# The first routed tile's up-projections placed between layer 0's last averages, and its rows joined in a side step

## The chip, the cores and the metric

The kernel runs on one core of a Trainium2 chip. The core's engines work side by side, each on its own queue: TensorE (PE) multiplies matrices, VectorE (DVE) and ScalarE (ACT) do elementwise work and read results out of PSUM, GpSimd (POOL) copies within SBUF and issues gathers and scatters by DMA, SyncE (SP) issues most of the other DMAs. The metric is device time in microseconds (us); a lower time is better.

## The reference

The program is two layers on 2 x 2048 tokens of width 256, in float32. Each layer adds to x an attention and a feed-forward part, both computed from the same normalised input. Only layer 0 is touched by the change; cut to what matters, it is:

```python
xn = _layernorm(x)
# causal attention, one head of width 256
q, k, v = xn @ Wq.T + bq, xn @ Wk.T + bk, xn @ Wv.T + bv
attn = where(causal, -inf, q @ k.T) / sqrt(256)
att = softmax(attn) @ v
# experts: 8 routed ones (hidden width 512), of which each token uses 2, and 2 shared ones
scores = softmax(xn @ gate_w + gate_b)
weights, indices = top_k(scores, 2)
expert = lambda x, e: (silu(x @ w1[e] + b1[e]) * (x @ w2[e] + b2[e])) @ w3[e] + b3[e]
routed = sum(weights * expert(xn, indices))
x = x + att + mean_of_shared_experts(xn) + routed
```

Layer 1 has the same attention without biases but with an output projection, and in place of the experts a block that works on the 255 highest-scoring tokens of each sequence.

## The kernel before, in words

**Attention of layer 0.** The queries are cut into tiles of 128. A tile is written (b, i): sequence b, block i of 16. The order is (0,0) to (0,15), then (1,15) down to (1,0), so the last tiles are the shortest. For each tile `scores` multiplies queries and keys on PE in chunks of 512 keys into PSUM banks of the tags `sc` and `tr` (two buffers each), DVE masks and shifts them (L264, L266), ACT takes the exponential (L274). Then `turn` transposes the probabilities without PE: POOL splits each float32 into two 16-bit planes (`planes`, L305), SP has a DMA transpose them (`across`, L307), and `join` puts the halves together again, one on DVE (L285) and one on ACT (L286), giving `pT`. `average` multiplies `pT` by the values on PE (L320), in a bank of the tag `pv`, and DVE adds the result to x (L330). Averages run some tiles behind their scores, in the list `pending`; when all tiles are scored, three are left: (1,2), (1,1) and (1,0). The loop `for late in pending` does these three.

**Side work.** Between pieces of the attention, `beside` takes steps of a generator, `side0`: it normalises the later blocks (`prepare0`), routes the tokens (`route_experts`), scatters the rows of all tokens to `sorted_x` in the order of their experts, and fetches the weights and rows of the first two routed tiles (`fetch(0)`, `fetch(1)`). In the last part of the attention it takes 0.72 steps a piece.

**Routed experts.** A tile is 256 places of `sorted_x` that belong to one expert; eight half tiles of 128 take what is left over. `fetch(t)` loads the expert's number into a register (L652), has SP transpose the rows by DMA into `xs` (L657), and loads the weights `rw1`, `rw2`, `rw3` (L665) and the biases `be` (L669), each with two buffers. `run(t)` joins the two 16-bit halves of the rows into `xT` on POOL (L765), and multiplies: for each of two pairs of hidden chunks a group of four products with `w1` into a bank `sc` and a group of four with `w2` into a bank `tr` (L772), four groups in all. ACT applies Silu (L780), DVE multiplies (L781), giving `hid`, and the down-projection follows on PE (L788). `xT`, `act`, `hid` and `y` come from the pool `hp`, which is opened when the attention's pools are closed.

**The order of work.** The Python code traces the instructions in program order. A planner then simulates the program and sets the order of each engine's queue: what is ready first goes first, and of what is ready what was traced first. So an instruction can stand on its engine ahead of others that were traced before it: the load of tile 2's expert number, traced in `run(2)`, ran at 322.1 us, in the middle of the attention. `tc.add_manual_dep(i, other, order, ...)` fixes that i stays behind another instruction of its engine, and with `wait` in place of `order` i also waits for it across engines. `lead(i)` marks the last instruction of the main work on an engine, in `main`; `behind` ties what a side step traces to it: POOL's instructions wait for the marked DVE instruction, SP's stay behind the marked SP one. `chained` keeps the SP instructions of all fetches in their order among themselves.

Of the kernel before, what the change touches and what calls it, by code (L numbers as in the profile page):

```python
# [17 lines left out]
P = 128  # L18
# [7 lines left out]
TT = 256  # L26
# [24 lines left out]
def transformer_kernel(ctx: ExitStack, tc: tile.TileContext, a: dict, out: bass.AP):  # L51
# [15 lines left out]
    def bank(tag):  # L67
        return psum.tile([P, 512], F32, tag=tag, name=f"ps_{tag}")
# [40 lines left out]
    def lead(i):  # L109

        main[i.ins.engine] = i.ins
# [121 lines left out]
                nc.tensor.transpose(ps[:, j * P : (j + 1) * P], xn[:, j, c * P : (c + 1) * P], ident)  # L233
            evacuate(xnT[g][:, c, :], ps)

    def attention(pool, tiles, project_q, values, each, shifts=None):

        def scores(b, i):
            g0 = b * BPB
            qT = queries[g0 + i // 4]
            row = pool.tile([P, S], F32, tag="row", name="row")
            mx = small.tile([P, 4], F32, tag="mx", name="mx")
            n = (i + 1) * P  # L250
            chunks = [(c, min(512, n - c)) for c in range(0, n, 512)]
            for k, (c, w) in enumerate(chunks):
                ps = bank(("sc", "tr")[k % 2])
                for dc in range(2):
                    product = nc.tensor.matmul(  # L255
                        ps[:, :w],
                        lhsT=qT[:, dc, (i % 4) * P : (i % 4 + 1) * P],
                        rhs=xnT[g0 + k][:, dc, :w],
                        start=(dc == 0),
                        stop=(dc == 1),  # L260
                    )
                lead(product)
                if c + w == n:
                    nc.vector.tensor_add(ps[:, w - P : w], ps[:, w - P : w], tri)  # L264
                by = 1.0 / 16.0 if shifts is None else shifts[g0 + i // 4][:, i % 4 : i % 4 + 1]
                lead(nc.vector.tensor_scalar(  # L266
                    row[:, c : c + w], ps[:, :w], by, None,
                    op0=ALU.mult if shifts is None else ALU.add, op1=ALU.max, accum_out=mx[:, k : k + 1],
                ))
                piece()  # L270
            nmx = small.tile([P, 1], F32, tag="nmx", name="nmx")
            nc.vector.tensor_reduce(nmx, mx[:, : len(chunks)], AX.X, ALU.max, negate=True)
            total = small.tile([P, 1], F32, tag="total", name="total")
            lead(nc.scalar.activation(row[:, :n], row[:, :n], AF.Exp, bias=nmx, accum_out=total))  # L274
            inv = small.tile([P, 1], F32, tag="inv", name="inv")
            nc.vector.reciprocal(inv, total)
            return b, i, row, inv, chunks

        def join(k, w, across, turned):

            pT = pool.tile([P, 512], F32, tag="pT", name="pT", bufs=6)
            words = pT[:, :w].bitcast(U16).rearrange("p (n k) -> p n k", k=2)
            flat = across.rearrange("p b n -> p (b n)")
            for i in (
                nc.vector.tensor_copy(words[:, :, 1], flat[:, :w]),  # L285
                nc.scalar.copy(words[:, :, 0], flat[:, w : 2 * w]),  # L286
            ):
                tc.add_manual_dep(i.ins, main[i.ins.engine].name, order, reason="not before it is there")
            turned[k] = pT

        def piece():

            pieces[0] += 1
            while joins and joins[0][0] <= pieces[0]:
                join(*joins.pop(0)[1:])
            beside()

        def turn(b, i, row, inv, chunks):

            turned = [None] * len(chunks)  # L300
            for k, (c, w) in enumerate(chunks):
                halves = row[:, c : c + w].bitcast(U16).rearrange("p (n k) -> p n k", k=2)
                planes = pool.tile([P, 1024], U16, tag="planes", name="planes", bufs=4)
                for h in range(2):
                    nc.gpsimd.tensor_copy(planes[:, h * w : (h + 1) * w], halves[:, :, 1 - h])  # L305
                across = pool.tile([P, 8, P], U16, tag="across", name="across", bufs=4)
                lead(nc.sync.dma_start_transpose(across[:, : 2 * w // P, :], planes[:, : 2 * w]))  # L307
                joins.append((pieces[0] + LAG + k, k, w, across, turned))
                if len(joins) == 4:
                    join(*joins.pop(0)[1:])  # L310
            return b, i, turned, inv, chunks

        def average(b, i, turned, inv, chunks):
            g0 = b * BPB
            pv = bank("pv")
            for k, (c, w) in enumerate(chunks):
                while turned[k] is None:
                    join(*joins.pop(0)[1:])
                for j in range(0, w, P):
                    product = nc.tensor.matmul(  # L320
                        pv[:, :D],
                        lhsT=turned[k][:, j : j + P],
                        rhs=values[g0 + k][:, j // P, :D],
                        start=(c + j == 0),
                        stop=(c + j == i * P),
                    )
                lead(product)
                piece()
            xt = x_blocks[g0 + i // 4][:, i % 4, :]
            nc.vector.scalar_tensor_tensor(xt, pv[:, :D], inv, xt, op0=ALU.mult, op1=ALU.add)  # L330

        queries = {}
        pending, joins, pieces = [], [], [0]
        def meet(tile):

            each(*tile)
            g = tile[0] * BPB + tile[1] // 4
            if g not in queries:
                queries[g] = project_q(g)

        meet(tiles[0])
        for tile, later in zip(tiles, tiles[1:] + [None]):
            pending.append(turn(*scores(*tile)))
            if later:
                meet(later)
            while sum(len(p[2]) for p in pending[:-1]) >= 3:
                average(*pending.pop(0))
        for late in pending:
            average(*late)


    in_turn = [(0, i) for i in range(S // P)] + [(1, i) for i in reversed(range(S // P))]
# [11 lines left out]
    with ExitStack() as l0:  # L364
# [279 lines left out]
        def fetch(t):  # L644
# [30 lines left out]
            fetched[t] = *parts, be, xs  # L675
            yield

        def side0():
            for blocks in (range(1, BPB), range(BPB, NB)):
                yield from moments(blocks)  # L680
                for g in blocks:
                    yield from prepare0(g)
            yield from route_experts()
            rows_ctx.close()
            wp.append(experts_ctx.enter_context(tc.tile_pool(name="experts", bufs=2, side="right")))
            for t in range(2):
                yield from fetch(t)

        def before_tile(b, i):
            while values[b * BPB + i // 4] is None:  # L690
# [6 lines left out]
            for _ in work_of:  # L697
                pass
        side.append(side0())
        attention(work, in_turn, project_q0, values, before_tile, shifts)  # L700
        assert next(clearing, None) is None
        while side:
            step()
# [46 lines left out]
    with ExitStack() as moe:  # L750
        hp = moe.enter_context(tc.tile_pool(name="routed", bufs=2))

        def run(t):
# [3 lines left out]
                    pass  # L757
            w1, w2, w3, be, xs = fetched[t]
            b1, b2, b3 = be[:, 0:4], be[:, 4:8], be[:, 8:]

            xs = xs.rearrange("p c n -> p (c n)")[:, : 4 * n].rearrange("p (c n) -> p c n", n=n)
            xT = hp.tile([P, 2, TT], F32, tag="xT", name="xT", bufs=3)[:, :, :n]
            words = xT.bitcast(U16).rearrange("p c (n k) -> p c n k", k=2)
            for k in range(2):
                nc.gpsimd.tensor_copy(words[:, :, :, 1 - k], xs[:, 2 * k : 2 * k + 2, :])  # L765
            hid = hp.tile([P, 4, TT], F32, tag="hid", name="hid")[:, :, :n]
            for h in range(0, 4, 2):
                p1, p2 = bank("sc"), bank("tr")
                for ps, we_in in ((p1, w1), (p2, w2)):
                    for k in range(2):  # L770
                        for dc in range(2):
                            nc.tensor.matmul(  # L772
                                ps[:, k * n : (k + 1) * n],
                                lhsT=we_in[:, dc, (h + k) * P : (h + k + 1) * P], rhs=xT[:, dc, :],
                                start=(dc == 0), stop=(dc == 1),
                            )
                for k in range(2):
                    act = hp.tile([P, TT], F32, tag="act", name="act", bufs=3)[:, :n]
                    at, hc = slice(k * n, (k + 1) * n), slice(h + k, h + k + 1)
                    activated = nc.scalar.activation(act, p1[:, at], AF.Silu, bias=b1[:, hc])  # L780
                    nc.vector.scalar_tensor_tensor(  # L781
                        hid[:, h + k, :], p2[:, at], b2[:, hc], act, op0=ALU.add, op1=ALU.mult
                    )
# [762 lines left out]
```

## Time and profile before

| | us |
|---|---|
| median of 3 runs | 1515.09 |
| lowest and highest | 1513.61, 1515.64 |
| profiled execution | 1515.69 |
| its span, first to last instruction | 1514.0 |
| PE busy in the span | 1455.0 (96%) |
| DVE, ACT, POOL busy | 695.7, 440.3, 407.7 |
| first and last average of layer 0 start | 54.5, 346.6 |
| first and last up-projection of a routed tile start | 348.5, 702.7 |
| last down-projection of a routed tile starts | 706.2 |

The profile is of one execution. Its page gives the busy time of each engine, the span in 40 slices (each digit the busy tenths), the DMA queues, the chain of work that ended last, and groups of instructions by line with their count, busy time, mean duration in ns, the idle time of the engine before them and what ended it. The trace behind it can be asked for a stretch of time: busy time by engine, waits, or the instructions in order of time with their start and length, merged where an engine repeats one line. A product of float32 matrices shows as two PE records, so one `average` of three key blocks is "x6", and a group of four up-projections "x8". PEld is PE's load of the stationary operand; SPq is SP's queue, where a DMA's issue is seen.

### The profile page before, as it was taken

The numbers are of one execution on the slowest core, as the hardware profiler recorded it, in microseconds if no ns is written. First come the engines' busy times: TensorE is split into PE (matmuls) and PEld (weight loads), VectorE is DVE, ScalarE is ACT, GpSimd is POOL, SyncE is SP. The second block draws the span as 40 slices with busy tenths as digits, with TensorE's granted clock in tenths as the row PEclk, the third lists the DMA queues.
The fourth block names the chain that finished last, engine by engine and source line by source line (L and its number), as shares of the span: only waits on it lengthen the run. The fifth ranks groups of instructions, "written<-read, shape, count | busy, mean of one in ns | idle before, by whom it ended". The sixth has DMA issues, their size and how long they took to land.

```text
span 1514.0 us, 17838 instructions
## 1 busy us (share of the span) xinstructions
PE 1455.0 (96%) x5796; PEld 1032.3 (68%) x5796; DVE 695.7 (46%) x2068; ACT 440.3 (29%) x831; POOL 407.7 (27%) x597
## 2 busy tenths in 40 slices
PE   6999999998999999999999999999999998999998
PEld 4566666667888888886565656666675765676665
DVE  6347433342222222222433447767556468666344
ACT  2443343332111111111112121125614433344233
POOL 3554776522111111101201222122013123421132
PEclk9999999999999999999999999999999999999999
DMA  4844665575887989873101010220005345621154
GB/s 151 262 113 115 173 147 130 140 154 147 228 224 222 274 237 292 225 218 94 34 18 39 29 56 25 87 71 29 0 21 125 90 87 115 134 51 23 35 118 102
DMA packets 288528, 182.99 MB, mean 121 GB/s; under 512 B 190928, under 2 KB 263376, under 8 KB 288432
## 3 DMA queue, kind: packets, MB, share of 16 engines
q1 hardware_dynamic: 252608, 133.90, 35.8%
q10 hardware_dynamic: 28192, 27.06, 5.8%
q0 software_dynamic: 7632, 20.86, 4.4%
q8 instruction: 48, 0.79, 0.2%
q14 instruction: 48, 0.39, 0.1%
HBM read 93.14 MB, written 45.14 MB: 91 GB/s over the span
## 4 chain that ended last, share of the span: by engine, by line
PE 29%; issue 10%; DVE 7%; POOL 3%; DMA 2%; ACT 2%; POOLq 0%; ACTq 0%; DVEq 0%; SPq 0%
PE ps_tr L1413 6%; PE ps_sc L1413 6%; PE ps_pv L1432 5%; POOL planes L305 3%; DMA across<-planes 2%; PE ps_mm L1284 2%; PE ps_mm L1246 1%; DVE x L1443 1%; PE ps_sc L255 1%; PE ps_mm L876 1%; PE ps_mm L1267 1%; PE ps_pv L320 1%; PE ps_mm L1350 1%; DVE row L266 1%; PE ps_tr L255 1%
## 5 line engine op out<-in xcount | busy, mean ns | idle before, releaser
L305 POOL COPY planes<-row 128x512 uint16<-128x512 uint16 (+3 forms) x320 | 167.1, 569 | 298.9 <-ACT row L274 289.2
L286 ACT COPY pT<-across 128x512 uint16<-128x512 uint16 (+3 forms) x160 | 106.1, 677 | 217.6 <-DMA across<-planes 206.7
L255 PE MATMUL ps_sc<-xnT,qT 128*128 128x512 f32 (+3 forms) x384 | 162.4, 544 | 0.5 <-ACT qT L624 0.5
L781 DVE SCALAR_TENSOR_TENSOR hid<-ps_tr,be,act 128x256 f32<-128x256 f32 (+1 forms) x144 | 61.0, 465 | 186.7 <-PE ps_tr L772 181.7
L1402 POOL DMA_INDIRECT ya<-sorted_y,place x64 | 62.3, 973 | 307.5 <-DVE x L1443 224.3
L780 ACT ACTIVATE act<-ps_sc,be 128x256 f32<-128x256 f32 (+1 forms) x144 | 58.8, 459 | 283.3 <-PE ps_sc L772 283.3
L320 PE MATMUL ps_pv<-v,pT 128*128 128x256 f32 x544 | 128.3, 381 | 6.1 <-ACT pT L286 4.7
L772 PE MATMUL ps_sc<-xT,rw 128*128 128x256 f32 (+1 forms) x576 | 129.5, 368 | 1.6 <-POOL xT L765 1.6
L320 PE MATMUL ps_pv<-vg,pT 128*128 128x256 f32 x544 | 125.1, 381 | 5.4 <-ACT pT L286 5.3
L772 PE MATMUL ps_tr<-xT,rw 128*128 128x256 f32 (+1 forms) x576 | 129.4, 367 | 0.0
L765 POOL COPY xT<-xs 128x512 uint16<-128x512 uint16 (+1 forms) x72 | 49.2, 728 | 293.3 <-DMA xs<-sorted_x 270.7
L788 PE MATMUL ps_pv<-rw,hid 128*128 128x256 f32 x544 | 124.9, 382 | 0.0
L1413 PE MATMUL ps_sc<-xnT,sw 128*128 128x512 f32 x256 | 121.9, 594 | 1.7 <-PEq L816 1.7
L1413 PE MATMUL ps_tr<-xnT,sw 128*128 128x512 f32 x256 | 122.0, 593 | 0.0
L320 PEld LDWEIGHTS ps_pv<-vg,pT 128*128 128x128 f32 x544 | 101.4, 189 | 29.7 <-ACT pT L286 10.3
L320 PEld LDWEIGHTS ps_pv<-v,pT 128*128 128x128 f32 x544 | 101.3, 190 | 28.2 <-ACT pT L286 8.2
L1432 PE MATMUL ps_pv<-sw,hid 128*128 128x256 f32 x512 | 117.5, 380 | 0.0
L772 PEld LDWEIGHTS ps_sc<-xT,rw 128*128 128x128 f32 x576 | 105.3, 190 | 15.4 <-POOL xT L765 2.0
L772 PEld LDWEIGHTS ps_tr<-xT,rw 128*128 128x128 f32 x576 | 105.1, 190 | 13.2
L788 PEld LDWEIGHTS ps_pv<-rw,hid 128*128 128x128 f32 x544 | 99.0, 189 | 19.5 <-DVE hid L781 5.9
L1432 PEld LDWEIGHTS ps_pv<-sw,hid 128*128 128x128 f32 x512 | 96.6, 190 | 18.8 <-issue 6.2
L1420 ACT ACTIVATE act<-ps_sc,sb 128x512 f32<-128x512 f32 x64 | 43.9, 686 | 219.5 <-PE ps_sc L1413 206.4
(332 smaller groups left out, 1964.7 us busy)
## 6 DMA issues: line engine op xcount, KB each, us to landing
rw<-in_rw SPq DMA_DIRECT2D x108, 512.0 KB, 4.5
sorted_x<-zero ACTq DMA_DIRECT2D x13, 768.0 KB, 6.4
sorted_y<-y SPq DMA_DIRECT2D x32, 256.0 KB, 4.1
be<-biases SPq DMA_DIRECT2D x36, 132.0 KB, 4.3
table<-xn SPq DMA_DIRECT2D x8, 514.0 KB, 3.6
x<-in_x SPq DMA_DIRECT2D x8, 512.0 KB, 6.6
gains<-zero ACTq DMA_DIRECT2D x8, 512.0 KB, 3.6
gain<-gains SPq DMA_DIRECT2D x16, 256.0 KB, 2.7
```

Source lines behind the costliest of these rows:

```text
L255: product = nc.tensor.matmul(ps[:, :w], lhsT=qT[:, dc, (i % 4) * P : (i % 4 + 1) * P], rhs=xnT[g0 + k][:, dc, :w], start=(dc == 0), stop=( ...
L286: nc.scalar.copy(words[:, :, 0], flat[:, w : 2 * w]),
L305: nc.gpsimd.tensor_copy(planes[:, h * w : (h + 1) * w], halves[:, :, 1 - h])
L320: product = nc.tensor.matmul(pv[:, :D], lhsT=turned[k][:, j : j + P], rhs=values[g0 + k][:, j // P, :D], start=(c + j == 0), stop=(c + j = ...
L765: nc.gpsimd.tensor_copy(words[:, :, :, 1 - k], xs[:, 2 * k : 2 * k + 2, :])
L772: nc.tensor.matmul(ps[:, k * n : (k + 1) * n], lhsT=we_in[:, dc, (h + k) * P : (h + k + 1) * P], rhs=xT[:, dc, :], start=(dc == 0), stop=( ...
L780: activated = nc.scalar.activation(act, p1[:, at], AF.Silu, bias=b1[:, hc])
L781: nc.vector.scalar_tensor_tensor(hid[:, h + k, :], p2[:, at], b2[:, hc], act, op0=ALU.add, op1=ALU.mult)
L788: product = nc.tensor.matmul(po[:, r, :], lhsT=hid[:, hc, r * P : (r + 1) * P], rhs=w3[:, hc, :], start=(hc == 0), stop=(hc == 3),)
L1402: nc.gpsimd.indirect_dma_start(out=ya, out_offset=None, in_=sorted_y, in_offset=bass.IndirectOffsetOnAxis(ap=place[rank][:, t : t + 1], ax ...
L1413: product = nc.tensor.matmul(ps, lhsT=ww[:, dc, hc * P : (hc + 1) * P], rhs=xnT[g][:, dc, :], start=(dc == 0), stop=(dc == 1),)
L1432: product = nc.tensor.matmul(po[:, :D], lhsT=hid[:, hc, j * P : (j + 1) * P], rhs=w["sw3", n][:, hc, :], start=(hc == 0), stop=(hc == 3),)
```

## The change

A generator `fill_with_first` is passed to layer 0's attention. It yields four times; each time one group of four up-projections of routed tile 0 has been traced. The loop over the last averages takes one group ahead of each of (1,2), (1,1) and (1,0), and one after them. Each group's PE instructions stay behind the average before it, and the next average's first product stays behind the group. `run(0)` then finds its banks filled and begins with Silu. The rows of tile 0 are joined in one more step at the end of `side0`, into a buffer `xT` of the pool `experts` (where the weights are), with one buffer; from tile 1 on they are joined in `run(t)` as before. The PSUM tags and the products are the same.

```diff
-    def attention(pool, tiles, project_q, values, each, shifts=None):
+    def attention(pool, tiles, project_q, values, each, shifts=None, filling=()):
...
                         stop=(c + j == i * P),
                     )
+                    if c + j == 0 and filled_up:
+                        tc.add_manual_dep(product.ins, filled_up.ins.name, order, reason="the filling first")
...
-        for late in pending:
-            average(*late)
+        filling = iter(filling)
+        for late in [*pending, None]:
+            last, n = main[mybir.EngineType.PE], len(nc.cur_bb.bb.instructions)
+            filled_up = next(filling, None)
+            if filled_up:
+                for i in nc.cur_bb.bb.instructions[n:]:
+                    if i.engine == mybir.EngineType.PE:
+                        tc.add_manual_dep(i, last.name, order, reason="not ahead of its turn")
+                lead(filled_up)
+            if late:
+                average(*late)
...
+        def joined(pool, xs, n, bufs):
+            xs = xs.rearrange("p c n -> p (c n)")[:, : 4 * n].rearrange("p (c n) -> p c n", n=n)
+            xT = pool.tile([P, 2, TT], F32, tag="xT", name="xT", bufs=bufs)[:, :, :n]
+            words = xT.bitcast(U16).rearrange("p c (n k) -> p c n k", k=2)
+            for k in range(2):
+                nc.gpsimd.tensor_copy(words[:, :, :, 1 - k], xs[:, 2 * k : 2 * k + 2, :])
+            return xT
+
+        def up(we_in, h, xT, n, tag):
+            ps = bank(tag)
+            for k in range(2):
+                for dc in range(2):
+                    product = nc.tensor.matmul(
+                        ps[:, k * n : (k + 1) * n],
+                        lhsT=we_in[:, dc, (h + k) * P : (h + k + 1) * P], rhs=xT[:, dc, :],
+                        start=(dc == 0), stop=(dc == 1),
+                    )
+            return ps, product
+
+        def fill_with_first():
+            while side:
+                step()
+            w1, w2, _, _, xT = fetched[0]
+            for h in range(0, 4, 2):
+                for we_in, tag in ((w1, "sc"), (w2, "tr")):
+                    first_up[h, tag], product = up(we_in, h, xT, TT, tag)
+                    yield product
...
             for t in range(2):
                 yield from fetch(t)
+            *others, xs = fetched[0]
+            fetched[0] = *others, joined(wp[0], xs, TT, 1)
+            yield
...
-        attention(work, in_turn, project_q0, values, before_tile, shifts)
+        attention(work, in_turn, project_q0, values, before_tile, shifts, fill_with_first())
...
+            if t:
+                xT = joined(hp, xs, n, 3)
...
+                p1, p2 = (
+                    up(we_in, h, xT, n, tag)[0] if t else first_up[h, tag] for we_in, tag in ((w1, "sc"), (w2, "tr"))
+                )
```

More of the change, by code (lines that the diff above doesn't have):

```diff
@@ L333, in attention @@
         pending, joins, pieces = [], [], [0]
+        filled_up = None
         def meet(tile):
@@ L347, in attention @@
                 average(*pending.pop(0))
-        for late in pending:
-            average(*late)
+        filling = iter(filling)
[9 more added lines that the diff above has]
+                average(*late)
+        assert next(filling, None) is None
     in_turn = [(0, i) for i in range(S // P)] + [(1, i) for i in reversed(range(S // P))]
@@ L676, in fetch @@
             yield
+        def joined(pool, xs, n, bufs):
[15 more added lines that the diff above has]
+            return ps, product
+        first_up = {}
+        def fill_with_first():
[6 more added lines that the diff above has]
+                    yield product
         def side0():
@@ L759, in run @@
             b1, b2, b3 = be[:, 0:4], be[:, 4:8], be[:, 8:]
[L761 to L765, printed above, removed]
+            if t:
+                xT = joined(hp, xs, n, 3)
             hid = hp.tile([P, 4, TT], F32, tag="hid", name="hid")[:, :, :n]
             for h in range(0, 4, 2):
[L768 to L776, printed above, removed]
+                p1, p2 = (
+                    up(we_in, h, xT, n, tag)[0] if t else first_up[h, tag] for we_in, tag in ((w1, "sc"), (w2, "tr"))
+                )
                 for k in range(2):
```

## The prediction

> **What bounds the kernel now.** I read the page's slices first, then the costliest groups, then the seam between layer 0's attention and its routed experts: busy time by stretch, waits, and the timeline of each engine. From the page:
>
> ```profile
> PE   6999999998999999999999999999999998999998
> PEclk9999999999999999999999999999999999999999
> L772 PE MATMUL ps_sc<-xT,rw 128*128 128x256 f32 (+1 forms) x576 | 129.5, 368 | 1.6 <-POOL xT L765 1.6
> L788 PE MATMUL ps_pv<-rw,hid 128*128 128x256 f32 x544 | 124.9, 382 | 0.0
> ```
>
> PE is 96% busy, and the routed stage behind the seam has almost no idle time on PE: 1.6 us before the first product, nothing later. So a shift of that stage's start moves its end by as much; what follows (the shared experts) starts behind the routed stage on PE and keeps its own order. What can be won lies where PE has a hole. Busy time of a stretch that starts where average (1,3) has issued its last product (length, then PE, weight load, DVE, ACT, POOL; granted clock, DMA share, GB/s), and the waits around it:
>
> ```profile
> 341.15:348.54 7.39, 3.60 (x15) 2.03 (x13) 3.01 (x9) 1.84 (x6) 2.84 (x7) 1.00 0.13 27
> POOL xT L765 <- PE ps_pv L320: 4.5, 1, 4.5
> PE ps_pv L320 <- ACT pT L286: 2.6, 3, 1.4
> PE ps_sc L772 <- POOL xT L765: 1.6, 1, 1.6
> ```
>
> PE is busy for less than half of 7.39 us. It waits for the turned probabilities of the last small tiles, and then for POOL, whose first join of rows waits for the last average (the pool of `hp` lies where the attention's buffers were). The clock is full throughout, so closing the holes wins their length and no more. PE and ACT by time (start, length, ..., idle before and what ended it):
>
> ```profile
> 339.42 2.00 PE L320 MATMUL ps_pv<-vg,pT 128*128 128x256 f32 x8 [0.41 <-ACT pT L286]
> 342.25 1.56 PE L320 MATMUL ps_pv<-vg,pT 128*128 128x256 f32 x6 [0.83 <-ACT pT L286]
> 345.18 1.77 PE L320 MATMUL ps_pv<-vg,pT 128*128 128x256 f32 x6 [1.36 <-ACT pT L286]
> 348.54 1.99 PE L772 MATMUL ps_sc<-xT,rw 128*128 128x256 f32 x8 [1.59 <-POOL xT L765]
> 353.82 1.89 PE L772 MATMUL ps_tr<-xT,rw 128*128 128x256 f32 x8
> 355.55 3.67 PE L788 MATMUL ps_pv<-rw,hid 128*128 128x256 f32 x16
> 344.65 0.48 ACT L286 COPY pT<-across 128x256 uint16<-128x256 uint16 x1 [2.45 <-DMA across<-planes]
> 345.86 0.33 ACT L286 COPY pT<-across 128x128 uint16<-128x128 uint16 x1 [0.74 <-DMA across<-planes]
> 350.68 1.28 ACT L780 ACT_TABLE_LOAD   x1 [4.49 <-PE ps_sc L772]
> 351.98 0.84 ACT L780 ACTIVATE act<-ps_sc,be 128x256 f32<-128x256 f32 x2
> ```
>
> The rows of L320 are the averages (1,3), (1,2), and (1,1) with (1,0); a product is two records. The four groups of up-projections, 8 records each, run from 348.54 to 355.55.
>
> **The change, part by part.**
>
> *The four groups move up.* No product is added or removed. A group takes 1.73 us (353.82 to 355.55). The rest of the averages is 12 records; at the down-projection's pace (16 records in 359.05 - 355.55 = 3.50 us, the same shape) that is 2.6 us. From 341.15 PE now needs 14.40 us to 355.55 for 4 x 1.73 + 2.6 = 9.5 us of work: 4.9 us are holes. In the new order: group 1 from 341.15 to 342.88, average (1,2) to 344.18, group 2 to 345.91, (1,1) to 346.77, group 3 to 348.50, (1,0) to 348.93, group 4 to 350.66. Each average's input is there: the ACT halves of pT end at 342.19 (341.59 + 0.60), 345.13 and 346.19, before 342.88, 345.91 and 348.50. The PSUM banks of the groups are free: the last score tiles were read by 340.9. The weights of tile 0 were issued around 297.7 and are not waited for now. So PE could start the down-projection at 350.66: **-4.9 us**.
>
> *The gate behind them.* The down-projection needs `hid`, hence Silu. No row of before shows whether `act` in `hp` must wait for average (1,0), as the first join did; without that wait nothing is lost, with it: (1,0) ends about 349.15 (0.2 after its last issue), table load to 350.55, first Silu to 351.05, first `hid` to 351.53 (0.48 as at L781), and PE starts about 351.58 instead of 350.66. The other `hid` pieces follow every 0.40 us and PE uses one in 0.44, so it doesn't stall again; before, it lost about 0.05 there. Ends: **0 to +0.9**; I take **+0.9**, since the nearest row, another tile of the same pool, waited. Here the Trainium skill speaks against the change: "ScalarE: Activation LUTs", What ACT_TABLE_LOAD costs, puts a switch of tables at 1.283 us plus a drain of about 1.38. The row has 1.28 and the Silu 0.02 us behind it, but ACT had stood idle for 4.5 us before it. By the rule the gain would be about 2.6, by the row 4.0. I take the row: after the change too ACT stands idle for 3 us, from 346.19 to 349.2, ahead of the load.
>
> *The join of tile 0 becomes a side step.* Two POOL copies (1.43 us a pair) leave the seam, where they cost PE 1.59, already counted. Counting pieces and side steps, they are traced behind the scores of (1,5) and ahead of its planes, and wait for that row on DVE (318.67). POOL, SP, DVE, ACT and PE there:
>
> ```profile
> 320.07 1.86 POOL L305 COPY planes<-row 128x512 uint16<-128x512 uint16 x4 [0.18 <-ACT row L274]
> L652 SPq TENSOR_LOAD <-tile_expert x1: 627/627/627, 322.1 to 322.1; - x1
> 323.24 1.24 SPq L307 DMA_TRANSPOSE across<-planes  x1
> 328.19 0.70 DVE L285 COPY pT<-across 128x512 uint16<-128x512 uint16 x2 [2.75 <-DMA across<-planes]
> 328.25 0.77 ACT L286 COPY pT<-across 128x512 uint16<-128x512 uint16 x1 [1.77 <-DMA across<-planes]
> 329.62 2.04 PE L255 MATMUL ps_sc<-xnT,qT 128*128 128x512 f32 x4 [0.47 <-ACT qT L624]
> ```
>
> Tile 0's rows were fetched at 306.2 (landing takes 3.4), so the join doesn't wait for them. POOL is through with (1,6) at 319.88; the join pushes the planes of (1,5) from 320.07 to 321.3, 1.24 us. What hides it is SP: the first half's planes are ready at 321.24, yet its turn through DMA is issued at 323.24, as SP loads the expert of tile 2 until 323.05. 1.24 is under the 2.0 of slack, the second half has 2.7: **0**. Were that cover gone, it would cost 1.24 us in full, since behind that DMA stand ACT's pT copy, behind it on ACT the queries, and PE waits for these.
>
> *What the early join sets free.* `xs` has two buffers; the rows of tile 2 are fetched by SP as soon as the first is read (today the join ends 348.49, the fetch is issued 348.51). Now it is free at 321.3. The planner puts such work ahead where it is ready, as it did with the index load of tile 2. If the fetch (1.24 on SP) lands between the two turns of (1,5) or later, SP is idle from 325.9 to 327.7 to take it: 0. If it lands ahead of the first, that turn is issued 1.2 us later: 324.5, at about the time of the second one today. Ends **0 and +1.3**, and below nothing if the planner then puts the queries ahead of pT on ACT (-0.5, the wait at 329.62). I take **0**: the first half of (1,5) is ready at 322.5, before SP ends its index load.
>
> *Later.* The weights of tile 2 (SP, 354.02 on) wait for groups that now end 4 to 5 us earlier and move along; nothing queued behind them is early. Tile 1's join can run at 349.3 and isn't needed before 355. The list of averages with one more empty turn issues nothing, and layer 1 passes no filling.
>
> **Sum.** -4.9 + 0.9 = -4.0 us. The profiled execution took 1515.69 (span 1514.0 and 1.7 around it) and would take 1511.7; the median shown is 0.6 lower, so I forecast **1511.1**. A run of this kernel can be told from no change beyond about 0.2%, 3.0 us.
>
> **Rivals.**
> 1. *Silu isn't held by the last average* (or is set ahead of it): -4.9, 1510.2. For: the layout isn't visible; against: the join's 4.5 us. 15%.
> 2. *The fetch for tile 2 goes ahead of the turn of (1,5).* -4.0 + 0.5 to 1.3, 1511.6 to 1512.4. For: 328.19 to 329.62 is one chain without slack from DMA to PE; against: the turn is ready first by the trace's times. 22%, half of it short of 0.2%.
> 3. *The gain goes elsewhere, or the change doesn't do what it says*: the join comes behind the last planes (342.60) and PE stands at group 1 for 3 us with three averages behind it, or Silu pays the drain: 0 to -2.7, about 1513.7. For: the planner orders POOL by costs that I can't see; against: 4.6 us of idle POOL from 321.93. 11%.
> 4. *Slower.* The turns of (1,5) stand on SP behind the fetch for tile 2, and this behind a join that POOL does only after the planes of (1,4) (to 328.19): the fetch is issued at 329.7, the turn at 331.0, 7.7 us late, and every us reaches PE through the queries: -4.0 + 7.7, 1518.8. It decides once the turn is issued more than 4.0 us late, after 327.3. Against: the planner would have to misjudge POOL by 6 us. 12%.
>
> The forecast itself has 40%. **Faster** than 0.2% is it, rival 1 and half of rival 2: 0.66; **within** it the other half and rival 3: 0.22; **slower** 0.12. The range takes in rival 1 with 0.7 beyond it (queries first, and the scatter of runs, 1 us) and rivals 2 and 3: 1509.5 to 1515.2; it leaves out rival 4 and the edges. The forecast's own range is 1510.4 to 1511.8.
>
> **What would show it.** Right: from the end of (1,3) PE has no hole over 0.3 us until group 4 ends; one hole of 0.9 before the first down-projection, whose gap names `hid`; that start 4.0 us earlier than 355.55; the pair of join copies before 322 and the turn of (1,5) still at 323.2. Wrong: a fetch of `xs` on SP between 322 and 325 with more idle PE time before the scores of (1,3); a PE wait for xT at group 1; Silu's load right after its group, without a wait for the average (rival 1); or a shift at 355 that isn't there at the span's end.

## The result, and the profile after

The changed kernel takes 1509.82 us in the median of 16 runs (1507.02 to 1514.48), the kernel before 1513.65 in 16 runs beside it (1509.75 to 1517.16). The ratio is 0.9974, with a 95% interval of 0.9964 to 0.9985: 3.9 us less, between 2.3 and 5.4. The forecast was 4.0 us less. Its absolute figure, 1511.1, started from the median of the first three runs before, 1515.09, which lies 1.4 above that of sixteen; so the measured median is 1.3 under it and 0.6 under the forecast's own range, though within the wide one of 1509.5 to 1515.2.

The profiled execution has a span of 1505.5 us, 8.5 below the one before. Most of that is not the change's doing: the last down-projection of a routed tile starts at 703.62 us after 706.20, 2.6 earlier, and layer 1's first average at 1140.55 after 1143.19, still 2.6. The other 5.8 us appear inside layer 1, which is the same in both; the last section says from what. First and last start of the down-projections, before and after:

```profile
L788 PE MATMUL ps_pv<-rw,hid x544: 379/379/431, 355.6 to 706.2; 128*128 128x256 f32 x182
L828 PE MATMUL ps_pv<-rw,hid x544: 379/379/431, 353.4 to 703.6; 128*128 128x256 f32 x182
```

PE at the seam, from the timeline of the kernel after (start, length, what, idle before and what ended it; L321 are the averages, L256 the scores of (1,3), L706 the up-projections, L828 the first down-projection):

```profile
325.66 3.19 PE L321 MATMUL ps_pv<-vg,pT 128*128 128x256 f32 x14
331.08 2.04 PE L256 MATMUL ps_sc<-xnT,qT 128*128 128x512 f32 x4 [2.23 <-ACT qT L638]
...
340.87 2.00 PE L321 MATMUL ps_pv<-vg,pT 128*128 128x256 f32 x8 [0.41 <-DVE x L333]
342.70 1.89 PE L706 MATMUL ps_sc<-xT,rw 128*128 128x256 f32 x8
344.43 1.46 PE L321 MATMUL ps_pv<-vg,pT 128*128 128x256 f32 x6
345.72 1.89 PE L706 MATMUL ps_tr<-xT,rw 128*128 128x256 f32 x8
347.45 1.03 PE L321 MATMUL ps_pv<-vg,pT 128*128 128x256 f32 x4
348.31 1.89 PE L706 MATMUL ps_sc<-xT,rw 128*128 128x256 f32 x8
350.04 0.59 PE L321 MATMUL ps_pv<-vg,pT 128*128 128x256 f32 x2
350.47 1.89 PE L706 MATMUL ps_tr<-xT,rw 128*128 128x256 f32 x8
352.94 0.67 PE L706 MATMUL ps_sc<-xT,rw 128*128 128x256 f32 x2 [0.58 <-issue]
353.44 3.62 PE L828 MATMUL ps_pv<-rw,hid 128*128 128x256 f32 x16
```

The groups and averages alternate without a hole; busy time by stretch shows PE busy for all of 9.60 us, where it was busy for 3.60 of 7.39:

```profile
342.60:352.20 9.60, 9.60 (x46) 8.24 (x44) 2.88 (x9) 3.34 (x8) 2.81 (x7) 1.00 0.18 32
```

Two things in the first listing were not in the forecast's sum. The wait ahead of the scores of (1,3) grew from 0.47 to 2.23 us. And the hole ahead of the down-projection is partly filled: the planner set the first product of tile 1 (x2) there. The other engines at the same time:

```profile
319.51 1.43 POOL L698 COPY xT<-xs 128x512 uint16<-128x512 uint16 x2
323.00 1.24 SPq L671 DMA_TRANSPOSE xs<-sorted_x  x1
324.42 1.24 SPq L308 DMA_TRANSPOSE across<-planes  x1
329.70 0.78 ACT L287 COPY pT<-across 128x512 uint16<-128x512 uint16 x1 [3.28 <-DMA across<-planes]
...
350.70 1.28 ACT L820 ACT_TABLE_LOAD   x1 [2.95 <-PE ps_pv L321]
352.00 1.57 ACT L820 ACTIVATE act<-ps_sc,be 128x256 f32<-128x256 f32 x4
```

The join runs where it was placed. Behind it the fetch of tile 2's rows stands on SP at 323.00, where the turn of (1,5) was issued before (323.24); the turn goes out at 324.42. Silu's table load waits for the last average, and the Silu follows the load after 0.02 us.

### The profile page after: what moved, and what is told of

Same layout as the page of the kernel before. It is cut to its first block, busy times and chain, and to the rows that moved or that the text cites. A ratio compares the mean times of both kernels' runs of the same rounds, so it can differ in the third digit from the quotient of the medians.

```text
span 1505.5 us, 17837 instructions
## 1 busy us (share of the span) xinstructions
PE 1448.6 (96%) x5796; PEld 1029.9 (68%) x5796; DVE 695.7 (46%) x2068; ACT 440.0 (29%) x831; POOL 407.6 (27%) x597
## 4 chain that ended last, share of the span: by engine, by line
PE 29%; issue 10%; DVE 7%; POOL 3%; DMA 2%; ACT 2%; POOLq 0%; ACTq 0%; DVEq 0%; SPq 0%
PE ps_tr L1453 6%; PE ps_sc L1453 6%; PE ps_pv L1472 5%; POOL planes L306 3%; DMA across<-planes 2%; PE ps_mm L1324 2%; PE ps_mm L1286 1%; DVE x L1483 1%; PE ps_sc L256 1%; PE ps_mm L916 1%; PE ps_mm L1307 1%; PE ps_pv L321 1%; PE ps_mm L1390 1%; DVE row L267 1%; PE ps_tr L256 1%
## 5 line engine op out<-in xcount | busy, mean ns | idle before, releaser
L256 PE MATMUL ps_sc<-xnT,qT 128*128 128x512 f32 (+3 forms) x384 | 161.1, 541 | 2.3 <-ACT qT L638 2.2
L321 PE MATMUL ps_pv<-v,pT 128*128 128x256 f32 x544 | 128.1, 381 | 5.5 <-ACT pT L287 4.5
L706 PE MATMUL ps_sc<-xT,rw 128*128 128x256 f32 (+1 forms) x576 | 129.6, 368 | 0.6 <-issue 0.6
L706 PE MATMUL ps_tr<-xT,rw 128*128 128x256 f32 (+1 forms) x576 | 129.4, 367 | 0.0
L321 PE MATMUL ps_pv<-vg,pT 128*128 128x256 f32 x544 | 124.5, 380 | 3.6 <-ACT pT L287 3.2
L828 PE MATMUL ps_pv<-rw,hid 128*128 128x256 f32 x544 | 124.9, 382 | 0.0
L321 PEld LDWEIGHTS ps_pv<-vg,pT 128*128 128x128 f32 x544 | 101.8, 189 | 26.6 <-ACT pT L287 6.9
L321 PEld LDWEIGHTS ps_pv<-v,pT 128*128 128x128 f32 x544 | 101.3, 189 | 27.3 <-ACT pT L287 8.0
L706 PEld LDWEIGHTS ps_sc<-xT,rw 128*128 128x128 f32 x576 | 105.3, 190 | 14.3 <-POOL xT L698 0.9
L706 PEld LDWEIGHTS ps_tr<-xT,rw 128*128 128x128 f32 x576 | 105.1, 190 | 13.2
L828 PEld LDWEIGHTS ps_pv<-rw,hid 128*128 128x128 f32 x544 | 99.2, 190 | 19.3 <-DVE hid L821 5.7
L256 PEld LDWEIGHTS ps_sc<-xnT,qT 128*128 128x128 f32 x384 | 69.9, 190 | 56.2 <-issue 43.1
```

The costliest lines, as they stand in the source:

```text
L256: product = nc.tensor.matmul(ps[:, :w], lhsT=qT[:, dc, (i % 4) * P : (i % 4 + 1) * P], rhs=xnT[g0 + k][:, dc, :w], start=(dc == 0), stop=( ...
L321: product = nc.tensor.matmul(pv[:, :D], lhsT=turned[k][:, j : j + P], rhs=values[g0 + k][:, j // P, :D], start=(c + j == 0), stop=(c + j = ...
L706: product = nc.tensor.matmul(ps[:, k * n : (k + 1) * n], lhsT=we_in[:, dc, (h + k) * P : (h + k + 1) * P], rhs=xT[:, dc, :], start=(dc == ...
L828: product = nc.tensor.matmul(po[:, r, :], lhsT=hid[:, hc, r * P : (r + 1) * P], rhs=w3[:, hc, :], start=(hc == 0), stop=(hc == 3),)
```

## The experiments

One stretch serves as the measure: from the start of average (1,6) to the start of the last down-projection. It is 380.24 us before and 377.96 after, and free of what differs from run to run ahead of it and in layer 1. Split at the start of average (1,3) it falls into two parts with different causes. All runs (times in us; "issue" is when the turn of (1,5) goes out, counted from the start of average (1,6); "landing" is from that issue to DVE's copy of it, since ACT's copy sometimes comes later because ACT is busy):

| run | fetch ahead of turn | issue | landing | PE wait before scores (1,3) | (1,6) to (1,3) | (1,3) to last down-projection |
|---|---|---|---|---|---|---|
| before | no | -2.72 | 4.95 | 0.47 | 13.46 | 366.78 |
| the change | yes | -1.24 | 5.23 | 2.23 | 15.21 | 362.75 |
| `pin` | no | -2.82 | 3.33 | 0 | 12.88 | 362.76 |
| `pin_table` | no | -2.50 | 3.87 | 0.15 | 13.21 | 362.01 |
| `join_only` | yes | -0.96 | 5.00 | 2.28 | 15.26 | 363.32 |
| `early_fetch` | yes | -1.40 | 3.35 | 0.19 | 13.18 | 366.88 |
| `spare_join` | no | -2.72 | 3.29 | 0 | 12.66 | 366.82 |
| `late_join` | yes | -1.12 | 5.11 | 2.22 | 15.20 | 362.75 |
| `table_only` | yes | -1.18 | 3.37 | 0.43 | 13.41 | 362.00 |
| `held` | no | -4.10 | 3.98 | 0 | 12.65 | 361.99 |

The right-hand column repeats within 0.1 us among kernels with the same seam. The part ahead of it doesn't, and follows the columns to its left: add issue and landing, and you have when the turn arrived, counted from the start of (1,6). In the six profiles in which PE waited 0.19 us or more, the wait is that arrival less 1.76 us, to 0.01. (In `pin_table` ACT was still busy with the tile (1,4) when the turn arrived.) So from before to after the wait grew by 1.76 us, of which 1.48 are the later issue and 0.28 the slower landing.

**The fetch of tile 2 held behind the last turn (`pin`).** In `fetch(t)`:

```diff
             if t > 1:
-                chained(turn)
+                i = chained(turn)
+                if t == 2:
+                    tc.add_manual_dep(
+                        i.ins, main[mybir.EngineType.SP].name, order, reason="behind the last turn"
+                    )
```

> The changed kernel, with the fetch of tile 2's rows held on SP behind the last DMA turn of the attention. Theory A (the early fetch costs 1.3 to 1.8 us, because the turn of (1,5) waits behind it on SP): the turn is issued straight after the index load, the hole on PE before the scores of (1,3) falls from 2.2 to about 0.5 us, and the stretch from the start of average (1,6) to the start of the last down-projection shortens from 377.96 to 376.2 to 376.7 us. Theory B (the join on POOL ahead of the planes of (1,5) is what delays it): the hole stays above 1.5 us and the stretch within 0.3 of 377.96. Against the kernel before, A gives a ratio near 0.9970, B what the change has.

Measured: 1510.02 us (16 runs) against 1514.17 before, ratio 0.9972 (0.9959 to 0.9985); the stretch 375.64. PE in this run:

```profile
324.72 3.19 PE L321 MATMUL ps_pv<-vg,pT 128*128 128x256 f32 x14
327.74 2.09 PE L256 MATMUL ps_sc<-xnT,qT 128*128 128x512 f32 x4
```

The wait is gone, which is theory A's direction and more than its size; the seam behind is unchanged (362.76). More than its size, since here the turn also landed sooner, 3.3 us after its issue where it took 5.0 before and 5.2 after the change. One run thus can't say how much the order on SP was worth.

**The early fetch alone (`early_fetch`).** The kernel before with `xs = wp[0].tile(..., tag="xs", name="xs", bufs=3)`.

> The kernel before with a third buffer for the fetched rows, so that tile 2's fetch can go out early; no join and no group is moved. Theory A (the early fetch on SP ahead of the turn of (1,5) has a price of its own): the wait of PE for the queries before the scores of (1,3) grows from 0.47 to about 1.7 to 2.2 us and the stretch from 380.24 to between 381.5 and 382.0. Theory B (it costs nothing by itself): 380.0 to 380.5.

Measured: 1515.54 (22 runs) against 1514.17, ratio 1.0009 (0.9996 to 1.0022); the stretch 380.06, the wait 0.19. By its numbers theory B holds and A missed. SP and PE:

```profile
323.37 1.24 SPq L657 DMA_TRANSPOSE xs<-sorted_x  x1
324.79 1.24 SPq L307 DMA_TRANSPOSE across<-planes  x1
329.56 1.61 PE L255 MATMUL ps_sc<-xnT,qT 128*128 128x512 f32 x3 [0.19 <-ACT qT L624]
```

The turn does go out behind the fetch, 1.3 us later against average (1,6) than before. But it landed after 3.4 us, and that hid the delay. So two terms make the wait, and the next runs were chosen to part them.

**The join alone, its result not used (`spare_join`).** The kernel before, with this at the end of `side0`:

```diff
+            xs = fetched[0][-1]
+            spare = wp[0].tile([P, 2, TT], F32, tag="xT", name="spare", bufs=1)
+            words = spare.bitcast(U16).rearrange("p c (n k) -> p c n k", k=2)
+            for k in range(2):
+                nc.gpsimd.tensor_copy(words[:, :, :, 1 - k], xs[:, 2 * k : 2 * k + 2, :])
+            yield
```

> The kernel before with a second, spare join of tile 0's rows in the side step, at the place where the change has its join; its result is not used, the rows stay needed by tile 0's own run, so no fetch can go out early and no group moves. It prices the 1.4 us on POOL alone. Theory A (SP's index load hides it): the turn of (1,5) is issued straight after the index load as before, the wait of PE before the scores of (1,3) stays under 0.6 us, and the stretch from average (1,6) to the last down-projection is 380.0 to 380.5 as in the kernel before. Theory B (POOL's delay makes the hole): a wait of 1.5 us or more and 381.5 or more.

Measured: 1515.29 (20 runs) against 1513.60, ratio 1.0010 (0.9999 to 1.0021); the stretch 379.48. POOL and SP:

```profile
320.32 1.43 POOL L692 COPY spare<-xs 128x512 uint16<-128x512 uint16 x2
321.66 1.86 POOL L305 COPY planes<-row 128x512 uint16<-128x512 uint16 x4
324.22 1.25 SPq L307 DMA_TRANSPOSE across<-planes  x1
```

The turn is issued 2.7 us ahead of average (1,6), as in the kernel before, though POOL did the planes behind the join, which takes 1.4 us: the first half was ready at about 322.83, before SP was through with its index load. The join is hidden, as forecast. The wait is 0, with a landing of 3.3 us; that quick landing is also why the stretch is 0.5 us shorter than the span that either theory named.

**The join set earlier, without its side step (`late_join`).** The change, with the join traced at the start of `fill_with_first` in place of the end of `side0`:

```diff
-            w1, w2, _, _, xT = fetched[0]
+            w1, w2, *others, xs = fetched[0]
+            xT = joined(wp[0], xs, TT, 1)
+            fetched[0] = w1, w2, *others, xT
...
-            *others, xs = fetched[0]
-            fetched[0] = *others, joined(wp[0], xs, TT, 1)
-            yield
```

> The change with its side step undone: the join is traced where the filling starts, into the same buffer, so nothing ties it to VectorE, and the planner sets it on POOL ahead of the planes of (1,7), about 8 us earlier than in the change; the fetch of tile 2 stands ahead of the turn of (1,5) on SP as in the change. Theory A (the order on SP makes the hole): the join now delays nothing of (1,5), yet the fetch still does; a wait of 1.5 us or more before the scores of (1,3) when the turn lands as slowly as in the change, and a stretch of 377.5 to 378.5. Theory B (it takes both, the join on POOL and the fetch on SP): a wait under 0.6 us and a stretch near 376. What happens to (1,7) lies ahead of the stretch.

Measured: 1511.97 (20 runs) against 1513.60, ratio 0.9987 (0.9977 to 0.9997); the stretch 377.95, as in the change to 0.01. SP and PE:

```profile
322.16 1.24 SPq L671 DMA_TRANSPOSE xs<-sorted_x  x1
323.58 2.61 SPq L308 DMA_TRANSPOSE across<-planes  x2
330.11 2.04 PE L256 MATMUL ps_sc<-xnT,qT 128*128 128x512 f32 x4 [2.22 <-ACT qT L638]
```

POOL had the planes of (1,5) ready at 319.97, 3.6 us before SP issued the turn, and the wait is the change's. With `spare_join` this settles it: the order on SP, not POOL, delays the turn. It also shows that a side step isn't needed for an early join: the planner pulled it ahead by itself. Its total gains less than the change's (0.9987 against 0.9974, with intervals that overlap), which the profiles don't show in layer 0: from the first average to (1,6) this run takes 270.8 us, the change 271.6.

**The groups not placed (`join_only`).** The change without `fill_with_first()`; tile 0's own run traces all four groups, with the early `xT`:

```diff
-        attention(work, in_turn, project_q0, values, before_tile, shifts, fill_with_first())
+        attention(work, in_turn, project_q0, values, before_tile, shifts)
...
-            if t:
-                xT = joined(hp, xs, n, 3)
+            xT = joined(hp, xs, n, 3) if t else xs
...
-                    up(we_in, h, xT, n, tag)[0] if t else first_up[h, tag] for we_in, tag in ((w1, "sc"), (w2, "tr"))
+                    up(we_in, h, xT, n, tag)[0] for we_in, tag in ((w1, "sc"), (w2, "tr"))
```

> The side-step join alone: the groups are traced in tile 0's own run again, nothing ties them to the averages. The early fetch is there as in the change. Theory A (the early join frees PE of its wait for POOL, and the planner then fills part of the holes by itself): the stretch from average (1,6) to the last down-projection is 0.3 to 1.0 us longer than in the change (378.3 to 379.0), against 380.24 before. Theory B (the placed groups make the gain): it is 380 or more, since the early fetch costs what the vanished wait for POOL brings.

Measured: 1510.92 (20 runs) against 1514.17, ratio 0.9979 (0.9967 to 0.9991); the stretch 378.58, in theory A's span. PE:

```profile
345.46 1.02 PE L706 MATMUL ps_sc<-xT,rw 128*128 128x256 f32 x4
346.46 1.56 PE L321 MATMUL ps_pv<-vg,pT 128*128 128x256 f32 x6
347.86 1.03 PE L706 MATMUL ps_sc<-xT,rw 128*128 128x256 f32 x4
349.37 1.89 PE L321 MATMUL ps_pv<-vg,pT 128*128 128x256 f32 x6 [0.48 <-ACT pT L287]
```

Once `xT` is early, the planner sets half a group ahead of (1,2) and half a group ahead of (1,1) by itself. From (1,3) on that run needs 363.32 us, the change 362.75, the kernel before 366.78: of the 4.0 us, 3.5 come with the early join, and the explicit placement adds 0.6.

**The table load early (`table_only`, `pin_table`).** In `fill_with_first`, in the change and in `pin`:

```diff
             w1, w2, _, _, xT = fetched[0]
+            warm = small.tile([P, 1], F32, tag="warm", name="warm", bufs=1)
+            i = nc.scalar.activation(warm, ones[:, 0:1], AF.Silu)
+            tc.add_manual_dep(i.ins, main[mybir.EngineType.Activation].name, order, reason="behind the last exp")
```

> As the run with the held fetch, and in addition one Silu of a single column behind the last exponential on ACT, so that the table load falls into ACT's idle time before the average (1,1). Theory A (Silu waits for the last average and the table load is then in the open): the load runs near 342 to 344 us, the first Silu starts within 0.2 us of the end of average (1,0), PE has no hole before the first down-projection, and the stretch is another 0.4 to 0.9 us shorter than in the run with the held fetch. Theory B (the wait for tile 0's memory, not the load, holds the down-projection): no shorter.

> The change with the early Silu of one column, the fetch of tile 2 left ahead of the turn of (1,5). Theory A: the table load alone is worth 0.4 to 0.5 us, so the stretch is 377.4 to 377.6 with the same wait before the scores of (1,3) as in the change (2.2 us), and correspondingly shorter when that wait is shorter; PE has no hole before the first down-projection. Theory B (the time of the run with both edits came from elsewhere): 378 with that hole still there.

Measured: `pin_table` 1508.15 (7 runs) against 1514.17, ratio 0.9945 (0.9923 to 0.9967), the stretch 375.21; `table_only` 1510.59 (13 runs) against 1513.60, ratio 0.9973 (0.9960 to 0.9986), the stretch 375.41. `pin_table` on ACT and PE:

```profile
342.95 0.61 ACT L287 COPY pT<-across 128x384 uint16<-128x384 uint16 x1
343.58 1.28 ACT L725 ACT_TABLE_LOAD   x1
344.88 0.20 ACT L725 ACTIVATE warm<-ones 128x1 f32<-128x1 f32 x1
...
350.62 1.56 ACT L827 ACTIVATE act<-ps_sc,be 128x256 f32<-128x256 f32 x4 [3.06 <-PE ps_pv L321]
350.37 1.89 PE L710 MATMUL ps_tr<-xT,rw 128*128 128x256 f32 x8
352.10 3.67 PE L835 MATMUL ps_pv<-rw,hid 128*128 128x256 f32 x16
```

Silu still waits for the last average, but starts at once when that is through, and the down-projection follows the fourth group without a hole. From (1,3) on both runs are 0.75 us shorter than the change (362.01 and 362.00 against 362.75), more than the 0.4 to 0.5 that I expected of the load alone. It is the hole of the change without the part that tile 1's first product had filled: the down-projection starts 1.24 us sooner behind (1,3), and that product (0.50) now comes later. The total of `table_only` doesn't show these 0.75 us; its interval is wider than that.

**SP left to the turns (`held`).** `pin_table`, with the load of tile 2's expert number (`values_load` in `fetch`) held in the same way, by an order dependency on the last turn for t == 2.

> The run with the held fetch and the early table load, in which the load of tile 2's expert number is held behind the last turn as well, so that SP has nothing but turns between (1,6) and (1,0). Theory A (SP's queue is what delays the turns here): the turn of (1,5) is issued as soon as its planes are ready, about 0.8 us earlier than with the fetch alone held, the wait before the scores of (1,3) is 0 to 0.2, and the stretch is 375.0 to 375.6: no gain over 375.21, since that wait is already gone. A ratio of 0.994 to 0.997 to the kernel before.

Measured: 1507.38 (6 runs) against 1513.60, ratio 0.9954 (0.9937 to 0.9971); the stretch 374.65. SP issues the turn at 320.83, 0.02 us behind its planes, 4.1 us ahead of average (1,6). The turn arrived 4.0 us later, when DVE copied it; ACT copied its half at 325.83, behind the exponential of the next tile, and PE didn't wait:

```profile
324.81 0.73 DVE L286 COPY pT<-across 128x512 uint16<-128x512 uint16 x2
325.00 0.83 ACT L275 ACTIVATE row<-row,nmx 128x640 f32<-128x640 f32 x1 [0.33 <-DVE nmx L273]
325.83 0.75 ACT L287 COPY pT<-across 128x512 uint16<-128x512 uint16 x1
```

The issue comes 1.3 us sooner than in `pin`, more than the 0.8 expected. By the sum above it would also cover a landing of 5.2 us (-4.10 + 5.23 is 1.13, under 1.76); that is an estimate, no such landing fell into this profile. The stretch is under the expected 375.0 to 375.6 and the shortest of all, 3.3 us under the change and 0.56 under `pin_table`, where no gain was expected. Its interval overlaps that of the change, so that it beats it is shown by the stretch, not by the total.

## Why the prediction was right, and where it was not

*The holes and the gate: right, in kind and size.* From the start of (1,3) to the last down-projection the kernel before needs 366.78 to 366.88 in three kernels, the changed seam 362.75 or 362.76 in three: -4.0, as forecast for the holes less the gate. With the table load moved away (`pin_table`, `table_only`, `held`) it is -4.8, nearly all of the 4.9. Most of the -4.0 needs only the early join, though: `join_only` has 3.5 of the 4.0, since the planner fills part of the holes without being told. Rival 1 (Silu not held) is refuted by the table load's 2.95 us of waiting for L321.

*The drain from the rule: not there.* In the change the Silu starts 0.02 us behind the load, but there ACT had stood idle ahead of it. `pin_table` shows a load without idle time: it starts 0.02 us behind the end of a copy, and the next instruction 0.02 us behind it. Counted from the start of average (1,0), the Silu comes at 1.96 us in the change and at 0.68 in `pin_table`: the difference is 1.28, the load alone. A drain of 1.38 us fits on neither side of it. The row was the right choice.

*The join on POOL at nothing: right.* `spare_join` and `late_join` show it from both sides. Its cover was the index load on SP.

*The fetch of tile 2 at nothing: wrong.* This is the step that failed. I argued that the turn is ready before SP ends its index load and so keeps its place. The planner decides by its own times, and it set the fetch first, in every kernel in which the buffer is free that early and nothing holds it; rival 2 is what happened, with the sign that I had named for it: a fetch of `xs` between 322 and 325 and more idle time before the scores of (1,3). I priced that at 0.5 to 1.3 us. The issue came 1.5 us later, and what of it reached PE depended on the landing: with a slow landing the wait went from 0.47 to 2.2 (1.8 us, above my bound), with a quick one from 0 to 0.2 or 0.4. The sign of being right that goes with it failed as well: the down-projection starts at 353.44, 2.1 us ahead of 355.55 and not 4.0.

*The sum.* On the stretch the change brought 380.24 - 377.96 = 2.3 us in the two profiled executions, both with a slow landing: -4.03 behind the start of (1,3) and +1.75 ahead of it. With quick landings it would be between -4.0 + 0.3 and -4.0 + 0.8: the part ahead takes 13.18 and 13.41 us with the fetch first (`early_fetch`, `table_only`) and 12.66 and 12.88 without (`spare_join`, `pin`). The measured 3.9 us (2.3 to 5.4) holds all of these, the 2.3 at its edge, so its nearness to the forecast 4.0 is in part luck and doesn't prove the zero for the fetch; the profile refutes it.

*Slower (rival 4)* needed a fetch that waits for a late join. The join ended at 320.94, before SP was free; the order on SP was the feared one, the wait in it was not.

## What to carry to other kernels

When an instruction is moved ahead, list which buffers it frees and which queued transfers may now start: here the fetch set free by an early join took the place of the one DMA that PE was waiting for, and gave back up to 1.8 of 4.0 us. A transfer that isn't needed soon is best tied behind those that are. Measure a seam by the time between two of its own instructions rather than by the total, when the rest of the program varies by more than the seam is worth.

## What the runs showed of the hardware

**The same DMA transpose lands quickly or slowly.** The turn of the first half of (1,5), identical in all ten profiles, reached DVE's copy 3.3 to 3.4 us after its issue in four of them, 3.9 and 4.0 in two, and 5.0 to 5.2 in four, whatever stood ahead of it on SP. The DMA queues of that stretch differ in one point. In the four slow ones (before, the change, `join_only`, `late_join`) a transfer of the queue of kind "instruction" (16 KB in one packet, of 0.9 to 1.2 us) starts between issue and landing; in the other six it doesn't. The DMA engines' busy tenths from issue to landing, before, with that queue's row (323.24 to 328.17), and in `spare_join`, which has no such row (324.22 to 327.48):

```profile
DMA  9975925553577999799997999000000000599600
q8 instruction: 1, 0.02, 1.2%
DMA  9999999999999116999999999999894149999996
```

Before, the packet started at 325.8, and from 326.3 on the DMA engines stood almost still for nine slices of 0.12 us. All ten profiles agree, but no run moved that transfer at will, so this cause is likely and not shown.

**The clock falls in layer 1 in some executions, and that makes most of the scatter.** Layer 1 has two places where PE has little to do. At the first, PE stood idle for 3.49 us before and 3.53 us after the change; busy time by stretch (the column after POOL's is the granted clock of PE) behind it, before and after:

```profile
1273.89 0.25 PE L1031 MATMUL ps_mm<-number,wrow 128*128 128x2 bf16 x4 [3.49 <-DVE wrow L1021]
1276.00:1278.00 2.00, 2.00 (x7) 0.78 (x6) 2.00 (x4) 0.00 (x0) 0.00 (x0) 0.50 1.30 184
1270.44 0.25 PE L1071 MATMUL ps_mm<-number,wrow 128*128 128x2 bf16 x4 [3.53 <-DVE wrow L1061]
1272.00:1274.00 2.00, 2.00 (x13) 0.88 (x12) 2.00 (x2) 0.00 (x0) 0.00 (x0) 1.00 1.37 132
```

At the second, in the block of the highest-scoring tokens, the same work before and after:

```profile
1397.34 0.93 PE L1267 MATMUL ps_mm<-ident,pr 128*128 128x128 f32 x4 [2.11 <-ACT pr L1258]
1398.94 3.78 PE L1284 MATMUL ps_mm<-wide,apart 128*128 128x256 f32 x8 [0.67 <-ACT wide L156]
1400.00:1402.00 2.00, 2.00 (x6) 1.64 (x5) 0.00 (x0) 0.00 (x0) 0.00 (x0) 0.50 0.00 0
1391.69 0.93 PE L1307 MATMUL ps_mm<-ident,pr 128*128 128x128 f32 x4 [1.83 <-ACT pr L1298]
1393.30 1.99 PE L1324 MATMUL ps_mm<-wide,apart 128*128 128x256 f32 x8 [0.68 <-ACT wide L156]
1394.00:1396.00 2.00, 1.92 (x11) 1.48 (x11) 0.56 (x2) 0.00 (x0) 0.00 (x0) 1.00 0.00 0
```

Before, PE ran at half its clock for 3.4 us at the first place and 6.8 us at the second (summed from the granted clock of such stretches), and the same eight products took 3.78 us instead of 1.99; after the change the clock stayed full at both. Some 10.2 us at half speed cost 5.1 us, an estimate that covers most of the 5.8. In the ten profiles layer 1's attention, from its first average to the end, takes 365.0 us at a mean clock over the whole span of 0.997, 366.9 to 367.4 at 0.995 and 0.996, 369.8 to 370.8 at 0.991 to 0.994, and 372.4 at 0.990.

The Trainium skill ("TensorE: Matmul & The Clock Gate", What's actually happening) has the clock go to half after an idle window of about 3.4 us. The first fall fits that, though after the change a hole of 3.53 us had no fall behind it; ahead of the second fall the longest hole was 2.11 us (with the transposes of L1267 behind it counted as idle, 3.1 us to the fall), so a single hole of that length wasn't needed. The instructions of layer 1 stand in the same order in all ten profiles, and the second fall is missing with the old seam in `early_fetch` and with the new one in the change, and there with the old one in the kernel before and with the new one in `pin`. So I take the falls as chance and not as an effect of the change; no run tested that.
